# A four-layer graph network on one core: what an opening does when its list of steps has run out

## The chip, the cores and the metric

The kernel runs on one core of one Trainium2 chip. The metric is the device time of one execution in microseconds (us); lower is better. The time before is the median of nine executions, and one further execution was taken with the hardware profiler.

## What is computed

Sixteen graphs share one adjacency matrix of 1024 nodes, in which an entry is set with probability 0.0078125, and have 128 features per node. Four layers follow each other. Layers 0, 2 and 3 are attention blocks:

```python
Q = (h @ Wq).reshape(B, N, NUM_HEADS, HEAD_DIM)      # K and V alike; 8 heads of 16
scores = jnp.where(mask, -jnp.inf, QK / sqrt(HEAD_DIM))   # mask: adj == 0
attn_out = softmax(scores) @ V
x = _layer_norm(h + (attn_out @ Wo + bo), ln1_g, ln1_b)
x = _layer_norm(x + relu(x @ W1 + b1) @ W2 + b2, ln2_g, ln2_b)
```

(shortened). Layer 1 is a graph attention with one score per edge, and a layer norm.

## The kernel before, in words

Since few entries are set, the kernel computes only on edges. It sorts the nodes by degree, puts 128 of them into each of eight tiles, and gives every tile a list of slots for neighbours. The graphs are handled in two groups of eight. A *unit* is one layer, one group and one tile (`units`, line 800: the tile runs fastest, then the group), so that layer 0 has units 0 to 7 for group 0 and units 8 to 15 for group 1.

For each layer and group there is a table in DRAM with the keys and values of all nodes. A unit reads rows of it with indirect DMAs that GpSimd (POOL) issues (`gathered`, line 905), four *parts* ahead. A part is a piece of a unit's slots: units 0 and 8 have seven parts, the other attention units five. For a part, VectorE (DVE) multiplies the gathered keys with the queries (`products`, line 917), sums over each head (line 940), ScalarE (ACT) takes exponentials (line 944), DVE weighs the gathered values (`weighted`, line 968), and TensorE (PE) adds up the slots of a node with matmuls against 0/1 marks (`summed`, line 984). Early in the next unit, DVE takes the reciprocal of the sums (`divided`, line 1021) and divides. I use these reciprocals as milestones: there is one for each unit. What follows for the divided rows (projection, layer norms, the feed-forward block, the table of the next layer) is the *tail* (`attention_tail`, `finish`, `project`), mainly PE and ACT work.

Python writes the instructions out in one order. Each engine then takes its own in that order, and waits on semaphores. The main loop over the parts writes down a part's own work, and between its stages it calls `others()`: such a call is an *opening* in which a little of some other work is written. There are three openings in an attention part: before the exponentials, after them, and at the end of the part. An opening first takes paced steps of the tails. Then it takes one step from one of three lists, the first that isn't empty:

- `fronts`: the queries of the next unit (`queries`: four steps and an end). For unit 0 the list begins with the rest of the edge lists (`slots`), `loaded(1)`, and the end of the weight loads.
- `loads`: the input of the unit after next (`loaded(u + 2)`). In layers 1 to 3 this is one DMA and is done at once. In layer 0 the input comes in two halves, h0 and h1: each is fetched by an indirect DMA from POOL (line 826), turned by four PE transposes (line 616, `ps<-ident,rows`), and copied by ACT (line 622). The generator's steps are: fetch h0; a pause; turn h0 and fetch h1; a pause; turn h1; end. The first step is taken in the unit's second part and the others in openings.
- `slow`: the projection of group 1's input to its table of layer 0 (`at_leisure`, `natural`, `project`). It comes in 16 *pieces*, k = 0 to 15, two for each tile. A piece is four transposes of `xg` (line 616), eight matmuls `ps<-Wkv,xT` (line 546), ACT copies (lines 622 and 550), and a table write from SyncE's queue (line 555). `idle()` gives this list unless a tail holds its place. A step of `loaded` that answers "idle" takes a step of it too.

Where an opening finds its generator at the end, it removes it and does nothing more. Two places force the rest: at the end of a unit the main loop runs `fronts` dry, and before the first gather of unit 8, the first to read group 1's table, `gathered` runs `slow` dry:

```python
        if u == T:
            while slow:
                advance(slow)
```

That gather waits for all table writes. `finish` also runs `slow` on until the piece at hand is complete, since both use the same buffer (`held`).

Of the kernel before, what the change touches and what calls it, by code (L numbers as in the profile page):

```python
# [126 lines left out]
def sparse_path(ctx: ExitStack, tc: tile.TileContext, a: dict, out: bass.AP, flag):  # L127
# [911 lines left out]
    fronts = []  # L1039
    loads = []  # L1040
# [4 lines left out]
    def advance(gens):  # L1045
        for gen in list(gens):
            got = next(gen, "end")
            if got == "end":
                gens.remove(gen)
            elif got == "free":  # L1050
                free.append(gen)
# [3 lines left out]
    def idle():  # L1055
        return slow if held[0] or not busy[0] else []

    def others():
        pace[0] += pace[1]
        while pace[0] >= 1.0:  # L1060
            advance(tails)
            pace[0] -= 1.0
        for gens in (fronts or loads or idle(),):
            if not gens:
                continue
            got = next(gens[0], "end")
            if got == "end":
                gens.pop(0)
            if got == "idle":
                advance(idle())  # L1070

    with tc.manual_schedule():
        wide = [gather_buffer() for _ in range(EDGES)]
# [36 lines left out]
        for i in range(len(parts) + 2):  # L1110
# [15 lines left out]
            if i > 1:  # L1126
                summed(i - 2)
                done = parts[i - 2][0]
                if parts[i - 1 : i] == [] or parts[i - 1][0] != done:
                    closing = divided(done)  # L1130
                    next(closing)
            others()
            if here:
                exponentials(i)
            if here and i == begun + 1:
# [7 lines left out]
                if u:  # L1143
                    advance(loads)
            others()
            if 0 < i <= len(parts):
                weighted(i - 1, 0)
                if not is_attention(parts[i - 1][0]):
                    others()
                    weighted(i - 1, 2)  # L1150
                gathered(i - 1 + AHEAD)
                for _ in sizes:
                    pass
# [454 lines left out]
```

## Time and profile before

| | |
|---|---|
| median of 9 executions | 2360.52 us (2352.21 to 2364.49) |
| the profiled execution's own time | 2342.46 us |
| its span, first to last instruction | 2340.7 us |
| granted TensorE clock, mean | 0.948 of full |
| busy: PE / DVE / ACT / POOL | 2062.0 / 1933.8 / 1530.6 / 1084.0 us |
| gathers of edges (line 905) | 600, busy 877.1 us on POOL |

The profiled execution lies 18 us below the median and is faster than all nine. Sums in this document are made against its span, and the difference is then added to the median.

The reciprocals of line 1021 stand in the timeline of DVE at these times, in us from the start of the span:

| unit | 0 | 1 | 2 | 3 | 4 | 5 | 6 | 7 | 8 | 9 | 10 | 11 | 12 | 13 | 14 |
|---|---|---|---|---|---|---|---|---|---|---|---|---|---|---|---|
| at | 189.28 | 237.78 | 280.37 | 321.81 | 365.34 | 407.87 | 450.10 | 502.14 | 546.45 | 583.04 | 619.63 | 656.51 | 693.16 | 729.77 | 766.36 |
| since the last | | 48.50 | 42.59 | 41.44 | 43.53 | 42.53 | 42.23 | 52.04 | 44.31 | 36.59 | 36.59 | 36.88 | 36.65 | 36.61 | 36.59 |

A profile is read like this: "busy" of an engine is the time in which one of its instructions ran; idle time is put down to the instruction or DMA whose semaphore came last. In a timeline, a row gives start, length, engine, line, operation, the tile written and the tiles read, and in brackets the idle time just before it with its releaser. Matmuls are shown with modelled ends, so that a row can overlap the next.

### The profile page before, as it was taken

To read this page: it belongs to the slowest core of one execution; us is meant where nothing else is said; L and a number is where in the kernel's file an instruction comes from. 1 tells how busy PE (TensorE), PEld (TensorE's weight loads), DVE (VectorE), ACT (ScalarE), POOL (GpSimd) and SP (SyncE) were. 2 spreads that over 40 slices of the span, in tenths; PEclk is the share of its full clock that TensorE was granted. 3 is DMA by queue.
4 is the path that set the end of the run, shared out by engine and by line. 5 is a ranking of instruction groups with operands and counts; after the bars stand their busy time and mean duration, and the time that the engine had idled before them with its cause. 6 is when DMAs were issued, how large, how long until landed. Compare 5 with 4: busy or idle time off the path is not lost. (4 is left out here: it accounts for less than half of the span.)

```text
span 2340.7 us, 36598 instructions
## 1 busy us (share of the span) xinstructions
PE 2062.0 (88%) x13124; PEld 1279.7 (55%) x13124; DVE 1933.8 (83%) x1486; ACT 1530.6 (65%) x5057; POOL 1084.0 (46%) x754
## 2 busy tenths in 40 slices
PE   6548899879999899998899999999999989898977
PEld 5415555545555555554466655666655555455544
DVE  7887786778989767777988989889898978989784
ACT  3215777766777656556577776877767767676765
POOL 3334453345545667885433344333444445454541
PEclk8768999999999999999999999999999999999998
DMA  7747787659778889999888887888878677676760
GB/s 251 241 156 244 258 303 276 247 208 317 278 274 290 259 283 361 334 366 334 286 294 284 300 311 258 320 290 303 315 257 304 230 283 267 246 259 258 254 246 25
DMA packets 168462, 636.05 MB, mean 272 GB/s; under 512 B 38329, under 2 KB 41145, under 8 KB 119775
## 3 DMA queue, kind: packets, MB, share of 16 engines
q0 software_dynamic: 92672, 485.09, 57.8%
q1 hardware_dynamic: 75600, 148.55, 18.9%
q8 instruction: 105, 1.72, 0.3%
q14 instruction: 85, 0.69, 0.1%
HBM read 603.11 MB, written 92.34 MB: 297 GB/s over the span
## 5 line engine op out<-in xcount | busy, mean ns | idle before, releaser
L905 POOL DMA_INDIRECT e<-table,idx x600 | 877.1, 1462 | 1051.5 <-DVE pr L968 850.9
L968 DVE TENSOR_TENSOR pr<-e,ex 128x2048 f32<-128x2048 f32 (+1 forms) x336 | 689.3, 2060 | 50.3 <-ACT ex L944 29.0
L917 DVE TENSOR_TENSOR pr<-e,qr 128x2048 f32<-128x2048 f32 x204 | 460.8, 2259 | 172.2 <-DMA e<-table,idx 84.5
L984 PE MATMUL acc<-pr,marks 128*32 128x512 f32 x2656 | 534.9, 614 | 53.9 <-DVE pr L968 43.1
L940 DVE TENSOR_REDUCE sc<-pr 128x128 f32<-128x2048 f32 (+1 forms) x252 | 518.5, 2057 | 8.6
L594 ACT ACTIVATE z<-yps,root 128x128 f32<-128x128 f32 x888 | 317.4, 388 | 38.7 <-PE yps L709 21.0
L984 PEld LDWEIGHTS acc<-pr,marks 128*32 128x32 f32 x2656 | 109.3, 111 | 304.4 <-issue 219.9
L705 PE MATMUL yps<-W,f 128*128 128x128 f32 x1520 | 250.8, 283 | 9.3 <-ACT f L700 5.2
L609 ACT ACTIVATE z<-yps,rstd 128x128 f32<-128x128 f32 x888 | 254.0, 369 | 7.2
L705 PEld LDWEIGHTS yps<-W,f 128*128 128x128 f32 x1520 | 205.0, 192 | 57.3 <-ACT f L700 28.5
L700 ACT ACTIVATE f<-ps,b 128x512 f32<-128x512 f32 x190 | 130.9, 693 | 156.7 <-PE ps L691 152.9
L546 PE MATMUL ps<-Wkv,xT 128*128 128x256 f32 x768 | 216.9, 423 | 17.0 <-ACT xT L622 9.5
L880 ACT COPY qr<-ps 128x512 f32<-128x512 f32 x384 | 197.2, 599 | 47.9 <-PE ps L877 47.4
L877 PE MATMUL ps<-q,rep 32*128 32x512 f32 x768 | 172.9, 665 | 39.7 <-ACT q L872 38.5
L594 ACT ACTIVATION_READ_ACCUMULATOR z<-yps,root 128x1 f32 x888 | 201.8, 227 | 0.0
L616 PE MATMUL ps<-ident,z 128*128 128x128 f32 x896 | 173.4, 295 | 32.0 <-ACT z L609 27.1
L944 ACT ACTIVATE ex<-sc 128x128 f32<-128x128 f32 (+1 forms) x252 | 79.6, 316 | 179.2 <-DVE sc L940 176.2
L616 PEld LDWEIGHTS ps<-ident,z 128*128 128x128 f32 x896 | 113.6, 141 | 150.5 <-ACT z L609 73.9
L546 PEld LDWEIGHTS ps<-Wkv,xT 128*128 128x128 f32 x768 | 147.9, 206 | 79.6 <-issue 21.6
L550 ACT COPY kv<-ps 128x512 f32<-128x512 f32 x176 | 103.6, 594 | 130.3 <-PE ps L546 104.6
L691 PE MATMUL ps<-x,W 128*128 128x512 f32 x384 | 186.5, 609 | 0.9 <-ACT x L624 0.9
L680 PE MATMUL yps<-Wo,oT 128*128 128x128 f32 x768 | 158.4, 289 | 9.9 <-ACT oT L622 9.7
(173 smaller groups left out, 2737.3 us busy)
## 6 DMA issues: line engine op xcount, KB each, us to landing
table<-kv SPq DMA_DIRECT2D x88, 512.0 KB
qx<-qr SPq DMA_DIRECT2D x96, 256.0 KB
kept<-xT SPq DMA_DIRECT2D x96, 256.0 KB
x<-kept SPq DMA_DIRECT2D x48, 512.0 KB
e<-table,idx POOLq DMA_INDIRECT x600
table<-kv SPq DMA_DIRECT2D x32, 256.0 KB
edges<-in_adj SPq DMA_DIRECT2D x8, 512.0 KB
spare<-in_x SPq DMA_DIRECT2D x8, 512.0 KB
```

The lines of the kernel that those rows point to most:

```text
L546: nc.tensor.matmul(ps[:, k, :], x[:, i + k, :], w[LAYERS[l][0], "Wkv"], start=True, stop=True,)
L594: nc.scalar.activation(z[:, i, :], y[:, i, :], AF.Square, scale=D**-0.5, bias=root, accum_out=total[:, i : i + 1],)
L609: nc.scalar.activation(z[:, i, :], y[:, i, :], AF.Copy, scale=rstd[:, i : i + 1])
L616: nc.tensor.transpose(ps[:, i, :], z[:, i, :], ident)
L691: nc.tensor.matmul(ps, p["W1"][:, f * P : (f + 1) * P], x1.rearrange("p g n -> p (g n)"), start=True, stop=True,)
L705: nc.tensor.matmul(ps[:, i, :], f1[:, f, i * P : (i + 1) * P], p["W2"][:, f, :], start=(f == 0), stop=False,)
L880: nc.scalar.copy(qs[u][:, j, h * GH * D : (h + 1) * GH * D], pss[j])
L905: nc.gpsimd.indirect_dma_start(out=es[i][:, k, :], out_offset=None, in_=tables[l, g][:, :], in_offset=bass.IndirectOffsetOnAxis(ap=idx[:, ...
L917: nc.vector.tensor_tensor(prs[i][0][:, :n, :], es[i][:, :n, :ROW], qx[u].rearrange("p (o c) -> p o c", o=1) if (MIX, 0) in piece else of_p ...
L940: nc.vector.tensor_reduce(sc[:, :n, :], prs[i][0][:, :n, :].rearrange("p k (a d) -> p k a d", d=HD), mybir.AxisListType.X, ALU.add,)
L968: nc.vector.tensor_tensor(prs[i][k0 // 2][:, :m, :].rearrange("p k (a d) -> p k a d", d=d), es[i][:, k0 : k0 + m, base : base + ROW].rearr ...
L984: nc.tensor.matmul(outs[32 * j : 32 * j + 32], marks[:, mark, :], rhss, start=(chunk == mine[0]), stop=(chunk == mine[-1]),)
```

## The change

In `others()`, the loop over one chosen list becomes a loop that goes on until a step has been taken or all lists are empty. A generator that is at its end is removed, and then the next one of the same list, or the next list, gives a step in the same opening. Nothing else is changed: the instructions are the same in number and kind, and only the places at which they are written differ.

```diff
         while pace[0] >= 1.0:
             advance(tails)
             pace[0] -= 1.0
-        for gens in (fronts or loads or idle(),):
+        while True:
+            gens = fronts or loads or idle()
             if not gens:
-                continue
+                break
             got = next(gens[0], "end")
             if got == "end":
                 gens.pop(0)
+                continue
             if got == "idle":
                 advance(idle())
+            break
```

## The prediction

> **What bounds the kernel now.** The change acts only while layer 0 runs group 0 and the first units of group 1, up to about 730 us, so I read the windows of single units first. Each goes from one reciprocal to the next: units 6, 7 and 9. The columns are the length, the busy time (and instructions) of PE, PEld, DVE, ACT and POOL, the granted PE clock, the DMA share and GB/s.
>
> ```profile
> core 0: us, PE busy (x) PEld busy (x) DVE busy (x) ACT busy (x) POOL busy (x), PEclk, DMA share, GB/s
> 407.87:450.10 42.23, 37.95 (x254) 24.84 (x253) 32.41 (x18) 31.18 (x104) 17.77 (x12) 1.00 0.77 271
> 450.10:502.14 52.04, 40.37 (x253) 26.91 (x253) 32.65 (x19) 31.63 (x104) 15.23 (x12) 0.93 0.62 218
> 583.04:619.63 36.59, 33.76 (x232) 21.33 (x230) 32.20 (x18) 28.09 (x99) 18.21 (x12) 1.00 0.80 277
> ```
>
> Unit 6 carries two pieces of the slow list, unit 9 none. The difference of 5.6 us makes 2.85 us a piece, close to the PE work in it (0.60 of transposes and 1.99 of matmuls): PE sets the pace. DVE, 32.2 busy, waits 3.21 at the reciprocal for PE's last sums. Unit 7 is 9.8 us longer than unit 6 with the same work. The timeline of unit 7, POOL, DVE and PE rows, shows why.
>
> ```profile
> 472.90 2.26 POOL L905 DMA_INDIRECT e<-table,idx  x1 [23.47 <-DMA table<-kv]
> 477.11 1.80 POOL L826 DMA_INDIRECT rows<-in_x,places  x1 [0.16 <-PE ps L616]
> 484.00 1.09 PE L616 MATMUL ps<-ident,rows 128*128 128x128 f32 x4 [6.82 <-DMA rows<-in_x,places]
> 484.88 1.06 PE L705 MATMUL yps<-W,f 128*128 128x128 f32 x4
> 488.44 0.61 PE L705 MATMUL yps<-W,f 128*128 128x128 f32 x4
> ```
>
> The first gather of unit 8 waits 23.47 us for the last table writes, pieces 14 and 15. POOL takes its instructions in order, so the fetch of h1 (line 826) stands behind it, and PE then waits 6.82 us for h1.
>
> Then I read the timeline of unit 9, POOL and PE, for the steps of `loaded`. The first two transposes of `z` and of rows there are h0's part of the order, the second two h1's.
>
> ```profile
> 596.73 0.99 POOL L826 DMA_INDIRECT rows<-in_x,places  x1
> ...
> 595.28 1.92 PE L984 MATMUL acc<-pr,marks 128*32 128x512 f32 x16
> 597.13 1.06 PE L616 MATMUL ps<-ident,z 128*128 128x128 f32 x4
> 598.03 0.60 PE L616 MATMUL ps<-ident,rows 128*128 128x128 f32 x4
> 598.56 1.91 PE L984 MATMUL acc<-pr,marks 128*32 128x512 f32 x8
> 600.40 1.98 PE L691 MATMUL ps<-x,W 128*128 128x512 f32 x4
> 602.22 0.60 PE L616 MATMUL ps<-ident,z 128*128 128x128 f32 x4
> 602.66 0.60 PE L616 MATMUL ps<-ident,rows 128*128 128x128 f32 x4
> ```
>
> h1 is issued at 596.73 and turned at 602.66, 5.9 us later, with no wait in the row. The four times that PE did wait for rows, its start lay 5.1 (145.01 to 150.12), 6.0 (187.28 to 193.29), 6.9 (477.11 to 484.00) and 5.3 us (515.83 to 521.16) after the issue began. The packets of POOL's queue put h1's landing in units without pieces at 18.6 to 19.6 us after the reciprocal, 13.7 of it before the issue: about 5 us, and PE starts some 0.4 later. So h1 arrives only about half a microsecond before it is used now.
>
> **What the skill says.** "TensorE: Matmul & The Clock Gate", "Step-by-step: what each phase is for": matmuls stay in program order, and only weight loads are pulled ahead. The trace agrees: at 484.00 everything behind the rows waits 6.82 us. The same page, Part 1: the clock drops to half after an idle window of about 3.4 us and returns after a busy one. It agrees: after the 6.82 us idle the same four matmuls take 1.06 us, and later 0.61. "DMA: Bandwidth & Descriptors", "Anatomy of one DMA — SWDGE (gpsimd) path": about 2.0 us and the bytes at 436 GB/s, which would be about 2.6 us for a fetch of 256 KB. The trace shows 5.1 to 6.9 us behind other gathers, and I use the trace.
>
> **The change part by part.** Comparing the written order of both programs, engine by engine, gives four effects. All instructions remain, none is added.
>
> *Pieces.* Whenever `queries` or `loaded` ends, the opening now gives the next list a step. Units 1 to 4 get three pieces each and unit 5 the last one; three are written by the reciprocal of unit 0, where there were two. None is left to be forced, and the writes end two units before the gather. The bubble, 52.04 less the 42.3 of a unit with two pieces, goes: −9.7. I see nothing late behind it, since unit 8's gathers then only wait for DVE to free a buffer. Moving a piece between units costs nothing in the sum, as PE sets the pace in both.
>
> *Units 0 and 1.* Here DVE waits 7.05 us at 176.90 for the queries of unit 1, and PE 6.53 at 193.29 for the rows of unit 2. The weights and `queries(1)` now come a part earlier, and on POOL the fetches for unit 2 stand two to three gathers ahead of where they stood. Unit 1 takes 48.50 where two pieces would need 42.3: I take all of these 6.2 back. Of the 7.05 I take back what pays for the extra piece (2.85) and 1.8 more. Sum −10.9, with bounds of −13 (both waits, 13.6, nearly whole) and +3 (only the piece comes on top).
>
> *The turn of h1.* In units 2 to 13, the steps of `loaded(u + 2)` all come one opening earlier. For PE this puts the turn of h1 ahead of the sums of 1.9, line 691's 1.98 and the `z` transposes. But POOL's order is unchanged there: the fetch of h1 stays at 13.7 us after the reciprocal, behind the gather that waits for DVE. In a unit without pieces PE comes to the rows at 597.13 + 0.53 for h0 + 0.5 for `z`, that is 598.2; h1 is there at 596.73 + 5.3 = 602.0. PE waits 3.8 us with all that stands behind: sums, line 691, the feed-forward block. PE and DVE meet within about half a microsecond at the unit's last sums (DVE's last product ends at 616.42), so little of the wait is absorbed, and I count 3.5. Bounds: 1.1 (a fetch that lands as fast as the skill's price of 2.6 us) and 5.4 (after 6.9, the longest seen); a gain is excluded, as nobody needs h1 before the next unit. The next unit's fetch is tied to its reciprocal and slides along, so the wait comes back in each unit. In units with pieces, two halves of line 546 (1.99) stand ahead of h1 in the new order: PE comes at 17.3 after the reciprocal, h1 at about 19.1; wait 1.8, and I count 2.0 since its fetch lands up to 0.7 later there. ACT's copies of h1 also move ahead of the `f` activations (line 700), which follow PE anyway: nothing. In unit 8 the order is another, with sixteen matmuls of lines 680 and 681 ahead of h1, and seven parts: +1.5.
>
> *The clock.* A wait of 3.8 us is about the idle window. After one short idle (unit 4, half clock from 361.84 to 365.26) a unit took 43.53 against 42.3: I take 1.2 us for a full wait, and half of that, 0.6, where the wait is 2.0. Bounds: 0, and 3 if two windows fall.
>
> The sum: u1 36.6 + 3 × 2.85 + 2.6 = 47.75, as u2, u3, u4; u5 36.6 + 2.85 + 2.6 = 42.05; u6 and u7 36.6 + 3.5 + 1.2 = 41.3; u8 45.8; u9 to u13 41.3 each. From 187.5 for unit 0 that gives 755.4 for the reciprocal of unit 13, against 729.77: +26. In parts: −9.7 bubble, −10.9 units 0 and 1, five units at 2.6 (+13), seven at 4.7 (+33), unit 8 +1.5, and −1 since units 2 to 6 ran a little over 42.3. After unit 13 `loaded` is one DMA, done at once, and nothing changes. The profiled execution took 2342.46 us, of which 2340.7 are its span; it becomes 2368.5. It lies 18.1 under the median of 2360.52, and I add the 26 to the median: 2386.5.
>
> **Rivals.**
>
> *Faster: the early turn is covered.* If fetches land some 2 us earlier in the new order, or DVE and ACT slack take the wait in, only the bubble and the start remain: −9.7 − 10.9 − 1 = −21.6, or 2339. For it: the fetch alone is priced at 2.6 us. Against it: landing 5 us or more after issue in every instance seen, with the DMA engines 0.77 to 0.80 busy. It decides at the point where the waits and the clock cost less than 21.6 over 13 units, 1.7 us a unit. Chance 0.12.
>
> *About even: half of it.* Waits without the clock effect, and 1.8 us in place of 3.5 (fetches moved up by feedback, or slack): 7 × 1.8 + 5 × 1.5 + 1 = +21, less 21.6: 2360. Chance 0.10.
>
> *More: nothing won at the start and longer drops of the clock.* Units 0 and 1 give nothing (+10.9) and the clock stays low for a second window in some units (+5): 2402. Chance 0.15.
>
> *It doesn't do what it says:* excluded by the order of the instructions; 0.01.
>
> **How the numbers follow.** The forecast, 2372 to 2396 about 2386.5, has 0.62. A measurement of this kernel can tell 0.2%, 4.7 us, from no change. Faster by more: rival one and a little of the second, 0.14. Within: 0.07, from the second rival. Slower: 0.79. The range of 8 in 10 leaves out rival one and the far end of the third: 2355 to 2405. The forecast's own range is 2372 to 2396.
>
> **What would show it.** The wait of 23.5 us for the table writes is gone, and unit 7 lasts 41 instead of 52. PE's waits at line 616 for rows, 19.0 us in 4 times now, come to about 14 times and 40 to 45 us, each some 3.8 us in units 6, 7 and 9 to 13 and about 2 in units 1 to 5. The reciprocals of units 9 to 13 stand 40 to 42 apart instead of 36.6, and from unit 14 on the distances are as before. The clock reads half for short stretches in units 6 to 13. I am wrong if the units 9 to 13 keep 36.6, if the fetch of h1 is issued earlier than 13.7 after the reciprocal, or if unit 1 stays at 48.5 or above.

## The result and the profile after

The changed kernel takes 2386.4 us (median of 10 executions, 2373.81 to 2397.52), against 2360.29 for the kernel before (31 executions). The ratio is 1.0108, with a 95% interval of 1.009 to 1.0126. The forecast was 2386.5.

The reciprocals of line 1021, as a table of milestones, show where the time went. "Unit" is the time since the reciprocal of the unit before, and "pieces" counts those that PE ran in it.

| unit | 1 | 2 | 3 | 4 | 5 | 6 | 7 | 8 | 9 | 10 | 11 | 12 | 13 | 14 |
|---|---|---|---|---|---|---|---|---|---|---|---|---|---|---|
| before, us | 48.50 | 42.59 | 41.44 | 43.53 | 42.53 | 42.23 | 52.04 | 44.31 | 36.59 | 36.59 | 36.88 | 36.65 | 36.61 | 36.59 |
| before, pieces | 1 | 2 | 2 | 2 | 2 | 2 | 2 | | | | | | | |
| after, us | 42.42 | 47.72 | 49.05 | 44.74 | 39.65 | 40.78 | 42.87 | 47.08 | 41.98 | 41.92 | 43.00 | 41.56 | 41.83 | 37.47 |
| after, pieces | 2 | 3 | 3 | 3 | 1 | 0 | 0 | | | | | | | |

(Unit 0 ends at 189.28 with three pieces before and at 189.19 with four after.) Unit 7 lost its bubble, units 9 to 13 grew by 4.9 to 6.1 us each, and the reciprocal of unit 14 moved from 766.36 to 791.26, by 24.9.

The windows of units 6, 7 and 10 of the changed kernel, with the columns as for the kernel before:

```profile
core 0: us, PE busy (x) PEld busy (x) DVE busy (x) ACT busy (x) POOL busy (x), PEclk, DMA share, GB/s
412.77:453.55 40.78, 35.29 (x231) 21.63 (x230) 32.39 (x19) 28.36 (x98) 17.80 (x12) 0.96 0.70 242
453.55:496.42 42.87, 36.67 (x230) 21.97 (x229) 32.40 (x19) 28.48 (x98) 17.80 (x12) 0.92 0.66 230
585.47:627.39 41.92, 35.46 (x231) 21.75 (x230) 32.39 (x18) 28.48 (x98) 17.84 (x12) 0.96 0.68 236
```

No piece is left in these units, and unit 7 is 9 us shorter than before. But unit 10 has the same instructions as in the profile before (the stretch 583.04:619.63, which the prediction calls unit 9; by the table it is unit 10) and takes 5.3 us more. PE's busy time grew from 33.76 to 35.46, though it has no more work, and its clock fell from 1.00 to 0.96.

The timeline of unit 10, POOL and then PE:

```profile
599.16 0.99 POOL L826 DMA_INDIRECT rows<-in_x,places  x1
...
600.47 0.65 PE L616 MATMUL ps<-ident,rows 128*128 128x128 f32 x4
600.96 0.60 PE L616 MATMUL ps<-ident,z 128*128 128x128 f32 x4
605.07 1.08 PE L616 MATMUL ps<-ident,rows 128*128 128x128 f32 x4 [3.51 <-DMA rows<-in_x,places]
606.08 3.12 PE L984 MATMUL acc<-pr,marks 128*32 128x512 f32 x8
609.13 1.98 PE L691 MATMUL ps<-x,W 128*128 128x512 f32 x4
```

The fetch of h1 starts 13.7 us after the reciprocal (599.16 − 585.47), exactly as before, and its data is used 5.9 us later, also as before. Only PE comes earlier, stands 3.51 us in front of it, and runs the next work at half clock: the sums take 3.12 in place of 1.91. In the list of PE's waits (total, times, longest) the kernel before had 19.0 us in 4 waits for rows; the changed one has

```profile
PE ps L616 <- DMA rows<-in_x,places: 45.7, 14, 8.2
```

and POOL's wait of 23.5 us for the table writes is gone from its list.

The profiled execution of before was 18 us shorter than the median, and the spans of the two profiles differ by 41.7 us. 17 us of that lie behind unit 14, where both kernels have the same order. I took two more traces of the kernel before to see whether this belongs to the change:

> The kernel before once more, for a second trace of it. Theory: the first trace was an execution with short later layers (1574 us from the reciprocal of unit 14 to the end, where six other kernels with the same later layers show 1583 to 1594), so this one shows some 1583 to 1594 there, and 766 for the reciprocal of unit 14. For the start: if what the change gains there is real, the reciprocal of unit 1 comes at 236 to 239; if it was variation, anywhere from 231 to 240.

> The same as the run before it, a third trace of the kernel before: 1583 to 1594 us behind the reciprocal of unit 14; the reciprocal of unit 1 at 236 to 239 if the gain at the start is real, at 231 to 240 if it was variation.

The stretch from the reciprocal of unit 14 to the end took 1582.1 and 1588.5 us (first trace 1574.3; changed kernel 1591.2). The first is 1 us short of what I expected, but the first trace was the outlier: the later layers vary by some 14 us between executions. In all fourteen traces of this document the stretch lies between 1574.3 and 1594.4 us, with a mean of 1586.1 in the six whose opening works as before or in part, and 1585.9 in the eight that hold the whole change, so no effect of the change shows in it. The reciprocal of unit 14 varies less in the kernel before: 766.4, 766.8 and 768.5, mean 767.2. I use it as the main yardstick below. That of unit 1 came at 234.8 and 236.1; the first lies outside what a real gain would show, so the second theory (variation at the start) holds; what follows from it stands under the run of the start alone.

### The profile page after: what moved, and what is told of

It reads as the page before. It is cut to its first block, busy times and chain, and to the rows that moved or that the text cites. A ratio compares the mean times of both kernels' runs of the same rounds, so it can differ in the third digit from the quotient of the medians.

```text
span 2382.4 us, 36595 instructions
## 1 busy us (share of the span) xinstructions
PE 2082.0 (87%) x13124; PEld 1281.7 (54%) x13124; DVE 1935.5 (81%) x1486; ACT 1535.1 (64%) x5057; POOL 1081.9 (45%) x754
## 5 line engine op out<-in xcount | busy, mean ns | idle before, releaser
L984 PE MATMUL acc<-pr,marks 128*32 128x512 f32 x2656 | 545.0, 623 | 48.1 <-DVE pr L968 39.7
L877 PE MATMUL ps<-q,rep 32*128 32x512 f32 x768 | 174.4, 655 | 42.9 <-ACT q L872 40.8
```

Of the source, the lines that this page charges most:

```text
L984: nc.tensor.matmul(outs[32 * j : 32 * j + 32], marks[:, mark, :], rhss, start=(chunk == mine[0]), stop=(chunk == mine[-1]),)
```

## Experiments

Where an edit adds lines ahead of line 984, the same line has a number higher by two in the rows shown. Ratios are to the kernel before on the same chip.

**h1 turned later.** From the changed kernel:

```diff
             yield "idle"
             yield "idle"
+            if u > 1:
+                yield "idle"
             turned(rows, xs[units[u]][:, 1])
```

> The changed kernel with one more pause ahead of the turn of h1 for units from 2 on, so that PE takes h1 again where it did before; the pieces and the start are those of the changed kernel. Theory (PE's early turn waits for the fetch): the waits for rows at line 616 fall from 14 times and 45.7 us to the two of the start (about 12 us), units 9 to 13 go back to about 36.6 us each, unit 7 is about 37, and the time is the one before less 21.6, some 2339 us (2331 to 2348). Rival (the turn of h0 and the copies of ACT, which stay early, cost the time): units 9 to 13 stay above 40 and the time is 2375 or more.

Measured: 2341.7 us, ratio 0.9948 (0.9932 to 0.9965). The waits for rows fell to 14.7 us in 3, units 9 to 13 took 36.4 us on average, and unit 7 36.8. So the early turn of h1 is the cost, and the turn of h0 with its copy on ACT, which stays early, is not. (ACT's copy of h1 belongs to `turned` and moves with the turn here; the run with h1 fetched earlier leaves it early.) The time lies inside what I expected, but beside the kernel before on the same chip the gain is 11 to 12 us, about half of 21.6. Unit 3 still took 48.6 us. Its PE rows (and the load on SyncE's queue, first row) say why:

```profile
297.70 0.33 SPq L750 DMA_DIRECT2D xg<-in_x  x1
...
305.22 0.63 PE L616 MATMUL ps<-ident,xg 128*128 128x128 f32 x4 [2.94 <-ACT kv L550]
305.78 3.60 PE L986 MATMUL acc<-pr,marks 128*32 128x512 f32 x8
```

The further pause gave the slow list its step one opening sooner. The input of the second piece, `xg`, was loaded only at 297.70, when its one buffer had come free, and PE stood 2.94 us at its turn, 7.5 us after the load was issued. The trace names ACT's copy `kv` as the releaser, but such a copy is not what feeds this turn; in unit 2 of this run a wait of 2.13 us at the same turn is put down to the load itself. That it is the load here too was an inference, which the next run tests.

**Two input buffers for the pieces**, from the run above:

```diff
-        rows = fetch(0)
+        rows = [fetch(0), fetch(1)]
...
-            steps = natural(g, k // HF, k % HF, rows)
+            steps = natural(g, k // HF, k % HF, rows[k % 2])
...
-            rows = fetch(k + 1)
+            rows[k % 2] = fetch(k + 2)
```

with a tag for each of the two buffers.

> The run with h1 turned later, and beside it two buffers for the input of the pieces, each loaded two pieces ahead in place of one (and two small buffers in place of three for the room). That run gained 12 us in place of 21.6, and its units 2 to 4 showed waits of PE at the turn of a piece's input of up to 2.9 us. Theory (with three pieces in a unit, the input of a piece is loaded too late): these waits are gone, unit 3 takes 44 to 45 in place of 48.6, and the ratio is 0.990 to 0.992. Rival (the rest of the forecast gain was never there): 0.994 to 0.996 as the run without it.

Measured: 2333.3 us, ratio 0.9913 (0.9886 to 0.9941). The waits for `xg` in units 2 to 4 are gone, and the gain is about the 21.6 us of the forecast. Windows of units 3, 5 and 11, with three pieces, one and none:

```profile
core 0: us, PE busy (x) PEld busy (x) DVE busy (x) ACT busy (x) POOL busy (x), PEclk, DMA share, GB/s
280.75:324.44 43.69, 39.54 (x265) 26.69 (x265) 32.30 (x19) 32.79 (x107) 18.38 (x12) 1.00 0.82 277
368.24:406.59 38.35, 35.52 (x241) 22.88 (x242) 32.41 (x19) 29.71 (x101) 18.38 (x12) 1.00 0.93 317
596.98:633.61 36.63, 33.30 (x230) 21.14 (x230) 32.21 (x19) 28.25 (x98) 17.03 (x13) 1.00 0.77 268
```

Three pieces lengthen a unit by 7.1 us and one by 1.7, while two lengthened it by 5.6 in the kernel before. PE's busy time grows by about 2.1 for each. So, set against the two-piece units of the kernel before, a third piece cost 1.5 us, not the 2.85 that I had from dividing by two.

**h1 fetched earlier, the order kept.** From the changed kernel:

```diff
             rows = fetch(0)
+            if u > 1:
+                other = fetch(1)
...
-            rows = fetch(1)
+            rows = other if u > 1 else fetch(1)
```

with a buffer of its own for h1, and two small buffers in place of three. The control has only the latter.

> The changed kernel with its order on PE and ACT kept, but from unit 2 on h1 is fetched right behind h0, some 11 us earlier, into a buffer of its own; to make room the pool of small tiles has two buffers in place of three. Theory (the wait is for late data): units 9 to 13 at 36.6 to 37.5 us, waits for rows only at the start, about 2340 us (2331 to 2350). Rival (the order itself costs, by what it puts ahead of ACT's and PE's other work): units 9 to 13 stay above 40, 2375 or more.

> Control for the run before: the changed kernel with two buffers in place of three in the pool of small tiles, and nothing else. If that pool is not a limit, 2386 us within 5 (ratio to the kernel before 1.009 to 1.013); if it is, slower by more, and the other run is to be read against this one.

The first took 2330.8 us, ratio 0.9891 (0.9859 to 0.9922), the control 2377.3, ratio 1.0085 (1.0054 to 1.0116), a little below the 1.009 to 1.013 expected: the small buffers are no limit. PE takes h0, `z` and h1 here in the order of the changed kernel. POOL and PE rows of h0 and h1 of unit 10 (the row of POOL is the fetch of h1, issued in unit 9):

```profile
550.31 2.91 POOL L826 DMA_INDIRECT rows<-in_x,places  x1 [0.30 <-PE ps L616]
...
570.16 0.66 PE L616 MATMUL ps<-ident,rows 128*128 128x128 f32 x4
571.09 0.60 PE L616 MATMUL ps<-ident,rows 128*128 128x128 f32 x4
```

With the fetch 20 us ahead, the same order costs nothing: units 9 to 13 took 36.7 us on average, PE waited for rows only twice, in unit 0, and the clock never fell in units 1 to 14. It is the age of the data that decides, not the order.

**The early turn alone**, in units 8 to 13 of the kernel before:

```diff
             yield "idle"
-            yield "idle"
+            if u < 10:
+                yield "idle"
             turned(rows, xs[units[u]][:, 1])
```

> The kernel before with one pause less ahead of the turn of h1 in units 8 to 13 alone, where no pieces are left: PE takes h1 one opening earlier, as in the changed kernel; the fetch stays. Theory: each of units 9 to 13 goes from 36.6 to about 42 with a wait of 3.4 for rows and half-clock windows of 3.4 us behind it, units 0 to 7 stay: 5 x 5.4 + 3 = 30 us slower, ratio 1.0127 (1.010 to 1.015). Rival (the waits are absorbed unless units 0 to 7 are also disturbed): below 1.004.

Measured: 2386.8 us, ratio 1.0145 (1.0104 to 1.0187). Units 9 to 13 took 41.5, 43.2, 41.5, 41.7 and 41.3, together 209.2 in place of 183.3, with waits for rows of 2.5 to 3.1 us; unit 8 took 1.0 more. The early turn is enough by itself, and in this stretch it costs 27 us. The rest of the median's 31 is within what the later layers vary.

**Pieces earlier, nothing else**, from the kernel before:

```diff
-            if got == "idle":
+            if got in ("idle", "end"):
                 advance(idle())
```

> The kernel before, with one thing of the change: an opening that finds a generator at its end takes a step of the slow list, and none of the other lists, so that pieces are written as early as in the changed kernel while queries, fetches and turns stay where they were. Theory: the 23.5 us wait of POOL for the table writes and with it 9.7 us of unit 7 are gone, units 9 to 13 stay at 36.6, and the first two units keep their waits: about 2351 us (2345 to 2357). Rival (the start was the larger gain, and pieces pushed earlier only lengthen units 1 to 5): 2358 to 2364.

Measured: 2336.6 us, ratio 0.9924 (0.9897 to 0.9951), so some 17 us faster, where I expected 10; the reciprocal of unit 14 came 13 us earlier than the mean of before (754.0). The wait for the table writes was gone, though PE waited 5.5 us for `xg` in three places, and 2.4 more at the same turn in unit 3 (put down to an ACT copy). Both the theory's 2351 and its rival's 2358 were too high, in part because the kernel before took 2353.1 us on this chip; but pieces alone are worth more than the bubble.

**The start alone**, from the kernel before (with the loop of the change):

```diff
             if got == "end":
                 gens.pop(0)
+                if fronts:
+                    continue
```

> The kernel before, in which an opening goes on to the next generator only while more than one is left in the first list, which is so at the start alone: the weights, the queries of unit 1 and the fetches for unit 2 come earlier as in the changed kernel, one piece of the slow list as well, and all units from 2 on keep their order. Theory: units 0 and 1 give some 11 us (6 to 13), the wait for table writes in unit 7 stays in good part, as the last piece is still forced there, units 9 to 13 stay at 36.6: ratio to the kernel before 0.995 (0.993 to 0.998). Rival (the gain at the start is variation between executions, and the pieces alone gave what was won): 0.998 to 1.001.

Measured: 2353.3 us, ratio 0.9987 (0.9966 to 1.0007): no gain. Unit 1 took 48.28, and the one piece left to be forced kept most of the wait. POOL's row in unit 7:

```profile
472.99 2.24 POOL L905 DMA_INDIRECT e<-table,idx  x1 [20.33 <-DMA table<-kv]
```

The 11 us of the theory lie outside the interval, and the rival holds; a gain of up to 8 us isn't excluded by the medians alone. Against it one might put the 42.42 of unit 1 in the changed kernel. But traces of the same start differ: the reciprocal of unit 1 came at 237.8, 234.8, 236.1 and 232.7 in four executions with the start of before, and at 231.6, 235.2, 235.8, 237.8, 237.4, 237.0 and 235.9 in seven with the start of the changed kernel. The means are 235.4 and 235.8; in the run of the start alone, not counted here, it came at 240.3. What the new start gives is not time but two pieces more, done by then (in the run of the start alone, one).

**The wait filled with work.** Right ahead of h1's turn, PE gets 24 transposes of the identity: first for the input of unit 2 and all after it, which puts them into units 0 to 13, and then in units 6 to 13 alone, beside the changed kernel on the same chip:

```diff
         ps = bank([P, GH, P])
+        for i in range(GH * fill):
+            nc.tensor.transpose(ps[:, i % GH, :], ident, ident)
```

> The changed kernel with 24 more transposes of the identity on PE, 2.6 us of work that nobody reads, right ahead of the turn of h1 in units from 2 on, so that PE works through most of its wait. Theory (a wait costs 3.4 by itself and about 1.8 more by the half clock behind it): the wait left for rows is about 0.8, no half clock in units 6 to 13, units 9 to 13 take 40.3 in place of 42.0, and with more work the kernel is faster, by about 1.7 x 9 = 15 us: ratio to the kernel before about 1.0045 (1.002 to 1.007). Rival (the wait alone costs, the clock nothing): 1.010 to 1.013 as the changed kernel.

> The changed kernel once more, as the base of the run behind it on the same chip: ratio to the kernel before 1.011 within 0.003; the reciprocal of unit 14 at 791 to 794 us; units 6 to 13 together 340 us.

> The changed kernel with the 24 idle transposes, 2.6 us of work, ahead of the turn of h1 in units 6 to 13 alone, where the wait was 3.4 and the half clock followed. Theory (the half clock costs about 1.8 a unit beside the wait): units 6 to 13 together 326 us in place of 340, and the kernel 14 us faster than the changed one on the same chip, with 5 us either way for the later layers. Rival (the clock costs nothing, and the shorter units of the first filled run were chance): no difference beyond 5 us, units 6 to 13 at 338 or more.

The first took 2373.3 us, ratio 1.0089 (1.0059 to 1.0119), an interval that reaches into both ranges: units 6 to 13 shrank from 341.0 to 326.4 (one of them, unit 9, still waited 2.18 us and had a half clock), but units 2 to 5 gained nothing from it. The pair settles it. The changed kernel again took 2380.0, ratio 1.012 (1.0094 to 1.0145); with filling in units 6 to 13 it took 2372.3, ratio 1.0074 (1.0057 to 1.0091). Units 6 to 13 fell from 341.1 to 325.8 us, 1.9 each. The whole gained 8 to 11 us of these 15; unit 4, which has the same order in both, took 3.6 us more in that execution, with a half-clock stretch in it. PE's rows of unit 10, and the window of unit 11:

```profile
600.91 0.60 PE L618 MATMUL ps<-ident,z 128*128 128x128 f32 x4
601.35 2.78 PE L616 MATMUL ps<-ident 128*128 128x128 f32 x24
605.16 0.66 PE L618 MATMUL ps<-ident,rows 128*128 128x128 f32 x4 [1.02 <-DMA rows<-in_x,places]
605.74 1.91 PE L986 MATMUL acc<-pr,marks 128*32 128x512 f32 x8
```

```profile
core 0: us, PE busy (x) PEld busy (x) DVE busy (x) ACT busy (x) POOL busy (x), PEclk, DMA share, GB/s
625.82:666.00 40.18, 36.33 (x254) 23.80 (x253) 32.39 (x18) 28.48 (x98) 16.94 (x12) 1.00 0.70 243
```

PE reaches h1 no later than before. What is saved is the half clock behind it: the sums take 1.91 again, the granted clock is 1.00, and a kernel with more work is faster.

## Why the prediction was right, and where its terms were off

The total was right for the reasons given in the main, a gain from pieces that come earlier and a larger loss from waits that come with h1; one part of the gain was booked in the wrong place, and there luck helped. Gain and loss can be parted, since the run with two input buffers has the pieces of the changed kernel without the waits. Its reciprocal of unit 14 stood at 743.25; before has 767.2 (mean of three traces) and the changed kernel 792.6 (mean of two).

| term | forecast | measured |
|---|---|---|
| gain: bubble, start, pieces | −21.6 | −24.0 (743.25 − 767.2) |
| loss: waits and clock | +47.5 | +49.4 (792.6 − 743.25) |
| sum | +26 | +25.4; medians +26.1 |
| loss up to unit 1 | 2.6 | −3.6 (233.4 against 237.0, the start varies) |
| loss of units 2 to 5 | 4 × 2.6 = 10.4 | 11.1 (180.7 against 169.6) |
| loss of units 6 and 7 | 9.4 | 9.7 (83.3 against 73.6) |
| loss of unit 8 | 1.5 | 2.7 (46.9 against 44.15) |
| loss of units 9 to 13 | 23.5 | 28.2 (210.9 against 182.7) |
| loss of unit 14 | 0 | 1.2 (37.5 against 36.3) |

The last six rows split the loss. With the other kernel without the waits, that with h1 fetched earlier (739.38), the gain is −27.8 and the loss +53.3. The 4 us between them come from ahead of the reciprocal of unit 1 (230.9 against 237.0), where executions vary; each row from units 2 to 5 on agrees within 1 us.

*The bubble* went as forecast, and nothing late took its place. Its size varies with the execution, and no run takes it away alone: unit 7 took 52.0, 54.0 and 54.4 us in the three traces of before.

*Units 0 and 1* were the step that failed. DVE's wait of 7.05 us for the queries is gone (0.52 are left, for a gather), but PE's wait for the rows of unit 2 is not. Before and after:

```profile
193.29 1.09 PE L616 MATMUL ps<-ident,rows 128*128 128x128 f32 x4 [6.53 <-DMA rows<-in_x,places]
175.34 1.11 PE L616 MATMUL ps<-ident,rows 128*128 128x128 f32 x4 [8.24 <-DMA rows<-in_x,places]
```

Before, PE waited for h1 of unit 2; in the changed kernel it waits for h0. The fetch of h0 moved up by 5 us (from 172.71 to 167.59), but PE was at its turn from 167.10 on, where before it came at 182.20 and didn't wait. The prediction counted that the fetches move up, but not that PE's turn moves up further: the same mechanism as in the later units. So by the reciprocal of unit 1 no time is won, only two pieces. The gain that I booked there exists all the same, in another place: the statement that moving a piece costs nothing in the sum was wrong, since a move can win time. Four pieces leave units 6 and 7, where each cost about 2.85. Two of them go into the waits of units 0 and 1, and two become third pieces in units 2 to 4. Units 2 to 5 took 170.1 us with eight pieces before, and 169.6 and 170.3 with ten in the two runs without waits. So by this sum about 11 us (4 × 2.85, an estimate) came from pieces that were absorbed, which is by chance the 10.9 that I had put down to the start. The count itself was off too, for both kernels: by the reciprocals of units 0 and 1, three pieces and one had run before, not two and two, and four and two after, not three and three. So the 6.2 us that I took back in unit 1 were set against a unit with one piece too many.

*The turn of h1* was right in mechanism, and in size in the units without pieces: waits of 3.2 to 3.7 us in units 7 to 13, and 2.5 in unit 6, against 3.8 seen ahead and 3.5 counted, with the issue at 13.7 in each. That all waits together, 14 times and 45.7 us, fit "about 14 times and 40 to 45" is in part chance: 12.2 us of them are the two of unit 0, and the twelve of units 2 to 13 come to 33.6. Units 2 to 5 came out right in the sum alone. The waits were 2.4, 3.5, 0.7 and 0.6 and not 2.0 each, with half-clock stretches behind the first two. In units 2 and 3 PE came at 18.3 and 18.5 us after the reciprocal, not 17.3, but h1 took 7.0 and 8.2 us from issue to use; in units 4 and 5 POOL issued the fetch at 11.9 and 12.4 us already, against the forecast, which had it fixed at 13.7. One of the four fetches that the prediction timed was read wrongly: counted in order, the rows of 193.29 are those of the fetch at 186.01, not 187.28, so they took 7.3 us and not 6.0, the longest of the four.

*The clock* was the term sized too small: 1.2 us a unit, where filling the wait gave back 1.9. The Trainium skill's "TensorE: Matmul & The Clock Gate", Part 1, says that the full clock comes back only after at least one busy window of about 3.4 us. Half of such a stretch, filled with matmuls, is 1.7, an estimate, and the records of the changed kernel show stretches of 3.4 and twice of 6.8 in units 6 to 13. The two units with 6.8 (7 and 11) are the longest, 42.9 and 43.0 against some 41.8. I had taken 1.2 from a unit with a single such stretch, whose 42.3 of comparison was itself a mean.

The rival of a covered turn, 2339, fell: fetches came sooner by themselves in units 4 and 5 only, where they left waits of 0.7 and 0.6, and nothing absorbed the wait in units 6 to 13. It does tell what the pieces are worth without the wait. Both kernels that mend it, the later turn with two input buffers and the earlier fetch, are faster than the kernel before and the changed one, with ratios of 0.9913 and 0.9891; their intervals overlap.

Why two pieces in a unit cost 5.6 us and three only 7.1 is a matter of PE's idle time, as its busy time grows evenly. The lists of PE's waits show most of it: one of a unit's pieces has its matmuls of line 546 written so soon behind its transposes that PE waits for ACT's copy `xT`, 1.1 us in unit 6 of the kernel before and 1.6 in unit 3 with two input buffers, while the other pieces there, and the one of unit 5, don't wait. So two pieces and three carry one such wait each. What stays open is why POOL issues the fetch early in units 4 and 5 of the changed kernel, and how much of the gain is the bubble and how much the absorbed pieces, which no run parts.

## What to carry to other kernels

When an instruction is moved up on an engine that works in order, look for how long its data has been there: here there was half a microsecond of margin or less in the units without pieces, and a move by some four microseconds turned it into a wait in each of a dozen units. A gain and a loss from one edit can be parted by moving the data early (or the consumer late) while the rest of the edit stays. Where TensorE sets the pace, as here, a wait can cost more than its length: 3.4 us of it, and 1.9 more by the clock that fell behind it.

## What the runs showed of the hardware that I had not expected

An idle time shorter than 3.4 us was enough for the half clock. In unit 2 of the changed kernel PE waited 2.38 us, and the sums behind it took 2.93 in place of 1.91:

```profile
252.26 0.63 PE L616 MATMUL ps<-ident,rows 128*128 128x128 f32 x4 [2.38 <-DMA rows<-in_x,places]
252.82 2.93 PE L984 MATMUL acc<-pr,marks 128*32 128x512 f32 x8
```

The clock records have half speed there for 3.4 us from 253.6. Behind a wait of 1.02 us, in the run filled in units 6 to 13, there was none. But length alone doesn't decide: in unit 2 of that same run PE waited 3.23 us, at 257.40, and the clock stayed full.

What tells the two apart is where the wait falls. In each trace the clock records change only at points that are multiples of 3.413 us apart. Cut at these points, the 2.38 us lie almost whole in one stretch (250.16 to 253.57, with PE busy for 39% of it), while the 3.23 us are divided between two (busy for 59% and 47%). In all fourteen traces, between the reciprocals of units 0 and 14, each of the 55 stretches at full clock in which PE was busy for less than 43% was followed by half clock, and of the 2238 others ten were. The 43% are read off these traces afterwards, and no run tests them; what sets the ten apart (62 to 65% busy) stays open, and in the later layers the line is less sharp (184 of 189, and 183 of 5805).

And 2.6 us of transposes that nobody reads, put into the waits of units 6 to 13, made the kernel 8 us faster (medians on the same chip).
